# An attention layer with a gated feed-forward, one core: the next batch's values due after its keys, other due times, shift rows moved between engines, and four smaller edits

## The chip, the cores and the metric

One core of a Trainium2 chip. TensorE (PE) multiplies matrices, VectorE (DVE), ScalarE (ACT) and GpSimd (POOL) work on rows, SyncE (SP) issues every transfer of this kernel. Each engine takes its instructions in the order of the program and waits on semaphores for the others. The metric is the device time of one execution in microseconds, the median of several runs; lower is better.

## The reference

x is 8 batches of 2048 tokens by 512 channels, all in fp32.

```python
xn = layernorm(x)
q, k, v = xn @ Wq.T + bq, xn @ Wk.T + bk, xn @ Wv.T + bv      # 8 heads: 8, 8 and 64 wide
scores = einsum("bmhd,bnhd->bhmn", q, k) / sqrt(8)
scores = where(scores >= 0, scores, 0.2 * scores)
s = gamma * (softmax(scores, -1) @ v) + xn
base = xn @ W.T
proj = l2norm(xn @ Wp.T + bp)
lw = softmax(proj @ l2norm(sim) * scale)                       # 4 experts, ranks 1, 2, 4, 8
res = sum over e of (lw[e] if e is the largest else 0) * (xn @ Wd[e].T @ Wu[e].T)
out = x + s * silu(base + res)
```

## The kernel before

**Main loop.** The work is cut into sequences of 16 steps. A sequence is one pair of heads (of 4) and one block of 512 query tokens (of 4) of one batch, so a batch has 16 sequences (`SEQ`) and the program 128 of them, 2048 steps. A step takes one chunk of 128 key tokens. On TensorE a step holds `less_max` (L621, adds the negative row maximum to the scores), `score` of the next step (L604), `max_unit` (L546, plain scores of the next sequence but one, for their row maxima) and `weigh` (L643, probabilities by values). ScalarE does `leaky` (L618, Prelu in place) and `exp` (L635), VectorE the maximum of `max_unit` (L568), GpSimd `add_up` (L661), which sums the probabilities. `less_max` of a step needs `leaky` of its scores, `exp` needs `less_max`. Up to four `weigh` calls are put off and wait in the list `last`.

**Background.** Everything else is written as Python generators that yield after small pieces, and `background` (L775) is called once a step to issue some of them. Queue 2 holds the work of `behind` (L753): `project_block` (L334) makes keys, queries and values of one block of the next batch, `lift_block` (L382) the gated feed-forward of one block of this batch. Queue 0 holds `ending` (L671), which finishes a sequence: sums, division, transposition, product and output. Queue 1 holds `shift_rows` (L570), which turns the row maxima of the next sequence into the rows that `less_max` adds. A generator that yields HOLD or WAIT keeps the one PSUM bank that all of them share, and the others stand back. FREE, SLOW and WAIT end the call; IDLE passes one step. Each piece calls `spend` with its planned cost (`MM` = 0.86 for a matmul with 512 columns).

**Due times.** `tasks` (L726 to L744) gives every block a planned cost and a due time in sequences, and `due_at` (L746) turns them into the cost that should be spent by a given step. `background` stops when `spent` reaches it. One batch in the order of the list: lift 1, lift 2, project 0, project 1, lift 3, project 2, project 3 and lift 0 of the next batch. The first seven are due at 13.4 sequences (`AHEAD`), the last at 16. In the last batch only three lifts are left, due at 13.2 (`LAST`).

**Where the plan meets the main loop.** `load_stacks(s + 2)` at step 0 of a sequence loads keys and queries of the sequence after the next. If they belong to the next batch, it calls `background(force=True)` until that batch is in `ready`, and `ready` is set after the values of its last block. `load_values(s + 1)` comes at step 6. `ending` waits in IDLE until its block is in `lifted`. All transfers go through SP's queue in program order: the stores of KS, QS, XN, XT, VS and GS, the loads of k, q_sb, v_sb, gs and xs, the shift rows and the output.

```python
while b > 0 and b not in ready:          # load_stacks
    background(force=True)
```

**Before the loop** a prologue makes batch 0's keys and values and the first half of its first lift.

Of the kernel before, what the change touches and what calls it, by code (L numbers as in the profile page):

```python
# [20 lines left out]
BLK = 512  # L21
NT = BLK // 128
# [3 lines left out]
SLOPE = 0.2  # L26
# [6 lines left out]
def fused_layer_kernel(  # L33
# [37 lines left out]
    nc = tc.nc  # L71
    B, M, C = x.shape
    NC = C // 128
# [67 lines left out]
    def filled(name, value, dtype=FP):  # L141
        c = const.tile([128, 1], dtype, name=name)
        nc.gpsimd.memset(c, value)
        return c

    hi_bits = filled("hi_bits", HI_BITS, I32)
    minus_one = filled("minus_one", -1.0)
    ln_eps = filled("ln_eps", LN_EPS)

    kst = []  # L150
# [89 lines left out]
    def spend(cost):  # L240
        spent[0] += cost

    def project(ps, wt, xnT):
        for c in range(NC):
            if c:
                yield HOLD
            nc.tensor.matmul(ps, lhsT=wt[:, c, :], rhs=xnT[c], start=(c == 0), stop=(c == NC - 1))  # L247
            spend(MM)

    def token_major(ps, wt, xnT, t, more=False):  # L250
        for c in range(NC):
            if c:
                yield HOLD
            nc.tensor.matmul(  # L254
                ps,
                lhsT=xnT[c][:, t * 128 : (t + 1) * 128],
                rhs=wt[:, c, :],
                start=(c == 0),
                stop=(c == NC - 1 and not more),
            )  # L260
            spend(MM)

    def columns(*tiles):
        return [a[:, c, :] for a in tiles for c in range(a.shape[1])]

    normed = {}
    ready = []
    lifted = []
    fetched = {}

# [63 lines left out]
    def project_block(b, n, following, prefetch):  # L334

        if (b, n) not in normed:
            for _ in norm(b, n):
                pass
        xn, normalize = normed.pop((b, n))
        xnT = two.tile([128, NC, BLK], FP, name="xnT")  # L340
        for t in range(NT):
            tp = bank([128, NC, 128], "tp")
            for c in range(NC):
                nc.tensor.transpose(tp[:, c, :], xn[:, t, c * 128 : (c + 1) * 128], ident)
            if t + 1 < NT:
                normalize(t + 1)
            nc.vector.tensor_copy(xnT[:, :, t * 128 : (t + 1) * 128], tp)
            spend(0.5)
            yield FREE
        if prefetch:  # L350
            fetch(*prefetch)
        nxt = b * NB + n + 2
        if nxt < B * NB:
            load_x(nxt // NB, nxt % NB)

        ps = bank([128, BLK], "qkps")
        yield from project(ps, wqk_sb, columns(xnT))
        nc.scalar.activation(ps, ps, AF.Identity, bias=bqk_sb)
        yield WAIT
        hi = one.tile([128, BLK], FP, name="hi")  # L360
        lo = one.tile([128, BLK], FP, name="lo")
        split_keys(b, n, ps, hi, lo)
        nc.sync.dma_start(out=XN[b][n], in_=xn)
        nc.sync.dma_start(out=XT[b][n], in_=xnT)
        yield FREE

        vb = one.tile([128, NPAIR, NT, 128], FP, name="vb")
        for t in range(NT):
            ps = bank([128, C], "vps")
            yield from token_major(ps, wv_sb, columns(xnT), t)  # L370
            add_bias(vb, t, ps)
            next(following, None)
            yield FREE
        store_values(b, n, vb)
        if n == NB - 1:
            ready.append(b)
        if not prefetch:
            for _ in following:
                yield FREE
            yield FREE  # L380

    def lift_block(b, n, following, prefetch, cols=None):  # L382

        early = cols is not None
        if not early:
            if (b, n) not in fetched:
# [4 lines left out]

        ps = bank([128, BLK], "pps")
        yield from project(ps, wp_sb, cols)
        pw = one.tile([128, 2, BLK], FP, name="pw")
        nc.vector.tensor_scalar(pw[:, 0, :], ps, bp_sb, None, ALU.add)
        nc.scalar.activation(pw[:, 1, :], ps, AF.Square, bias=bp_sb)
        yield FREE
        nps = bank([128, NT], "nps")
        for t in range(NT):
            nc.tensor.matmul(  # L400
                nps[:, t : t + 1],
                lhsT=pw[:, 1, t * 128 : (t + 1) * 128],
                rhs=ones[:, 0:1],
                start=True,
                stop=True,
            )
# [13 lines left out]
        for t in range(NT):  # L420
            nc.tensor.matmul(
                gps[:, t, 0:NEXP],
                lhsT=pw[:, 0, t * 128 : (t + 1) * 128],
                rhs=simn,
                start=True,
                stop=True,
            )
# [75 lines left out]
    def where(s):  # L503
        return s // SEQ, s % NPAIR, (s % SEQ) // NPAIR
# [28 lines left out]
    def load_values(s):  # L533
        if s >= B * SEQ:
            return
        b, p, n = where(s)
        vts[s] = two.tile([128, CH, 128], FP, name="v_sb")
        nc.sync.dma_start(out=vts[s], in_=VS[b][p])

# [30 lines left out]
    def shift_rows(s):  # L570
        if s >= B * SEQ:
            return
        m = sm.tile([128, 2 * NT, 1], FP, name="m")
        nc.vector.reduce_max(m, mxr.pop(s).rearrange("p e t n -> p (e t) n"), axis=AX.X)
        yield IDLE

        ml = sm.tile([128, 2 * NT], FP, name="ml")
        nc.scalar.activation(ml, m[:, :, 0], AF.Prelu, alpha=SLOPE)
        c = sm.tile([128, 2, 2 * NT], FP, name="c")
        big = sm.tile([128, 2 * NT], FP, name="big")  # L580
        nc.scalar.activation(big, ml, AF.Copy, scale=-4097.0)
        nc.scalar.activation(ml, ml, AF.Copy, scale=-1.0)  # L582
        nc.gpsimd.tensor_tensor(c[:, 1, :], big, ml, ALU.subtract)  # L583
        nc.gpsimd.tensor_tensor(c[:, 0, :], big, c[:, 1, :], ALU.subtract)
        nc.gpsimd.tensor_tensor(c[:, 1, :], ml, c[:, 0, :], ALU.subtract)
        for _ in range(2):
            yield IDLE
        yield FREE
        cps = ps_m.tile([4 * NT, 128], FP, name="cps", tag="m")
        nc.tensor.transpose(cps, c.rearrange("p i m -> p (i m)"), ident)  # L590
        cT = sm.tile([4 * NT, 128], FP, name="cT")
        nc.vector.tensor_copy(cT, cps)
        spend(0.45)
        shift = qp.tile([128, BLK], FR, name="shift")
# [76 lines left out]
    def ending(s):  # L671
# [4 lines left out]
        nc.vector.tensor_copy(avs, avt.pop(s))  # L676
        yield IDLE
        sums = acc.pop(s)
        for _ in range(2):
            yield IDLE  # L680
        while (b, n) not in lifted:
            yield IDLE
        gs = two.tile([128, NT, 128], FP, name="gs")
# [35 lines left out]
        nc.sync.dma_start(out=ov[b, n][:, :, cols], in_=gs)  # L719
        yield FREE  # L720

    AHEAD = 13.4
    LAST = 13.2


    A1, A2 = 20 * MM + 2.0, 24 * MM + 3.7  # L726
    tasks = [(lift_block, 0, 0, 16 * MM + 1.7, 1.4)]
    for b in range(B):
        order = [(lift_block, b, 1)]
        if b + 1 < B:  # L730
            order += [(lift_block, b, 2), (project_block, b + 1, 0), (project_block, b + 1, 1)]
            order += [(lift_block, b, 3), (project_block, b + 1, 2), (project_block, b + 1, 3)]
            order += [(lift_block, b + 1, 0)]
        else:
            order += [(lift_block, b, 2), (lift_block, b, 3)]
        costs = [A2 if f is lift_block else A1 for f, _, _ in order]
        t0 = tasks[-1][4]
        steady = sum(costs) - (costs[-1] if b + 1 < B else 0.0)
        t1 = SEQ * b + (AHEAD if b + 1 < B else LAST)
        run = 0.0  # L740
        for k, (f, bb, n) in enumerate(order):
            run += costs[k]
            end = t0 + (t1 - t0) * run / steady if run <= steady + 0.01 else SEQ * (b + 1.0)
            tasks.append((f, bb, n, costs[k], end))  # L744

    def due_at(h):  # L746
        w, t = h * END, 0.0
# [3 lines left out]
        return w  # L751

    def behind():  # L753
        for k, (f, b, n, _, _) in enumerate(tasks):
            g, bb, nn = (tasks[k + 1] if k + 1 < len(tasks) else (None, 0, 0))[:3]
            following = norm(bb, nn) if g is project_block else iter(())
            if k == 0:
                yield from opening
            else:
                yield from f(b, n, following, (bb, nn) if g is lift_block else None)  # L760
# [48 lines left out]
    with tc.manual_schedule():  # L809
# [144 lines left out]
        for s in range(B * SEQ):  # L954
            for i in range(CH):
                if i == 0:
                    load_stacks(s + 2)
                if i == 6:
                    load_values(s + 1)
                due[0] = due_at(s + (i + 1) / CH)  # L960
                u = s * CH + i + CH + LEAD
# [82 lines left out]
```

## Time and profile before

| | before |
|---|---|
| median of 3 runs | 5834.28 us (5829.07 to 5840.97) |
| profiled execution, whole | 5841.93 us |
| its span | 5840.2 us |
| mean granted clock of TensorE | 0.967 |
| TensorE busy | 5433.9 us |
| GpSimd busy | 4705.6 us |
| ScalarE busy | 4276.0 us |
| VectorE busy | 3620.9 us |
| first L626 (step 0) | 132.5 us after the start |

The profile is one execution, taken on the chip. Busy time is counted per engine; matmuls overlap, so their sum can be more than the busy time. The timeline gives the start and duration of instructions, how many of a kind follow one another (x2), and in brackets how long the engine had been idle and what ended it. A table of windows gives for each stretch its length, the busy time of PE, its weight loads, DVE, ACT and POOL with their instructions, the granted clock, the DMA share and GB/s. A matmul in fp32 shows as two instructions.

### The profile page before, as it was taken

Reading aid. Unit: us, or ns where it says so; the run is one execution under the profiler, and the core shown is the slowest. Engines: PE = TensorE matmul, PEld = TensorE weight load, DVE = VectorE, ACT = ScalarE, POOL = GpSimd, SP = SyncE. Lnnn points to the kernel's source line nnn. Section 1 sums busy time; section 2 is a strip of 40 time slices with the busy share of each in tenths; the row PEclk is TensorE's granted clock in tenths of the full one; section 3 lists DMA queues with packets and bytes.
Section 4 is the critical chain, followed back from the end, with each engine's and each line's share of the span. In section 5 each row is a group of like instructions: output and inputs, shape, how many; then the busy total and the mean of one; then the engine's idle time right before and its main releaser. Section 6 shows DMA issues by size and latency. Waiting matters only on the chain.

```text
span 5840.2 us, 74003 instructions
## 1 busy us (share of the span) xinstructions
PE 5433.9 (93%) x26242; PEld 1780.7 (30%) x26242; DVE 3620.9 (62%) x4716; ACT 4276.0 (73%) x4915; POOL 4705.6 (81%) x2519
## 2 busy tenths in 40 slices
PE   7899999999999999999999999999999999988888
PEld 3333333333333333333333333333333333322222
DVE  5566656666566666666666666666666666555552
ACT  2677767777777777777777777777777777767666
POOL 1788878888888888888888888888888888878777
PEclk9999999999999999999999999999999999988885
DMA  5233333334224242243423434233342334322221
GB/s 200 90 109 121 105 115 88 108 106 152 89 75 152 77 152 86 75 143 95 135 82 95 132 104 130 82 104 123 104 124 89 104 111 129 97 62 80 70 76 33
DMA packets 517991, 614.04 MB, mean 105 GB/s; under 512 B 30780, under 2 KB 429116, under 8 KB 481528
## 3 DMA queue, kind: packets, MB, share of 16 engines
q1 hardware_dynamic: 517624, 609.32, 33.6%
q8 instruction: 209, 3.42, 0.2%
q14 instruction: 158, 1.29, 0.1%
HBM read 405.79 MB, written 201.33 MB: 104 GB/s over the span
## 4 chain that ended last, share of the span: by engine, by line
PE 68%; ACT 21%; DVE 5%; POOL 2%; issue 2%; DMA 1%; SPq 1%; ACTq 0%; POOLq 0%; DVEq 0%
PE av L649 22%; PE sc L626 14%; ACT ex L637 10%; ACT sc L619 9%; PE zps L254 9%; PE vps L254 8%; PE mx L561 5%; PE dps L247 2%; PE pps L247 2%; PE qkps L247 2%; DVE mxr L568 2%; POOL acc L669 1%; ACT xn L292 1%; PE sc L609 1%; DVE bs L277 1%
## 5 line engine op out<-in xcount | busy, mean ns | idle before, releaser
L669 POOL TENSOR_TENSOR acc<-acc,ex 128x1024 f32<-128x1024 f32 x1792 | 4236.9, 2364 | 353.0 <-ACT ex L637 268.3
L568 DVE TENSOR_REDUCE mxr<-mx 128x2 f32<-128x1024 f32 x2048 | 2504.2, 1223 | 1814.3 <-PE mx L561 1798.2
L637 ACT ACTIVATE ex<-sc 128x1024 f32<-128x1024 f32 x2048 | 2097.6, 1024 | 1388.2 <-PE sc L609 1198.7
L649 PE MATMUL av<-ex,v_sb 128*64 128x512 f32 x8192 | 2228.5, 634 | 0.9 <-DVE avs L676 0.9
L619 ACT ACTIVATE sc<-sc 128x1024 f32<-128x1024 f32 x2048 | 2086.2, 1019 | 19.9 <-PE sc L609 19.9
L626 PE MATMUL sc<-shift,ones_r 2*128 2x512 f32 x4096 | 1055.6, 507 | 301.6 <-ACT sc L619 294.3
L609 PE MATMUL sc<-q_sb,k 32*128 32x512 f32 x4096 | 1044.8, 506 | 0.0
L626 PEld LDWEIGHTS sc<-shift,ones_r 2*128 2x128 f32 x4096 | 393.9, 185 | 2050.2 <-ACT sc L619 1947.2
L561 PE MATMUL mx<-k,q_sb 32*128 32x512 f32 x4096 | 831.5, 400 | 13.5 <-DVE mxr L568 13.5
L649 PEld LDWEIGHTS av<-ex,v_sb 128*64 128x64 f32 x8192 | 437.9, 138 | 954.9 <-issue 928.6
L669 POOL TENSOR_TENSOR acc<-ex 128x1024 f32<-128x1024 f32 x128 | 301.9, 2358 | 397.6 <-ACT ex L637 397.6
L254 PE MATMUL zps<-w_sb,xnT 128*128 128x512 f32 x1024 | 567.4, 656 | 12.1 <-DMA xnT<-XT 12.0
L254 PE MATMUL vps<-wv_sb,xnT 128*128 128x512 f32 x960 | 508.3, 633 | 6.8 <-DVE vb L322 2.3
L561 PEld LDWEIGHTS mx<-k,q_sb 32*128 32x128 f32 x4096 | 400.3, 190 | 35.3 <-DVE mxr L568 33.9
L609 PEld LDWEIGHTS sc<-q_sb,k 32*128 32x128 f32 x4096 | 386.6, 186 | 0.8 <-issue 0.8
L254 PEld LDWEIGHTS zps<-w_sb,xnT 128*128 128x128 f32 x1024 | 168.3, 195 | 254.0 <-issue 194.8
L254 PEld LDWEIGHTS vps<-wv_sb,xnT 128*128 128x128 f32 x960 | 153.8, 189 | 210.9 <-issue 176.5
L492 DVE SCALAR_TENSOR_TENSOR g<-th,zps 128x512 f32<-128x512 f32 x128 | 88.0, 688 | 166.9 <-ACT th L491 166.9
L583 POOL TENSOR_TENSOR c<-big,ml 128x8 f32<-128x8 f32 x128 | 26.1, 204 | 186.8 <-ACT ml L582 178.8
L247 PE MATMUL pps<-xnT,wp_sb 128*128 128x512 f32 x256 | 142.1, 646 | 5.6 <-DVE vb L322 5.5
L247 PE MATMUL dps<-xnT,wd_sb 128*128 128x512 f32 x256 | 146.3, 661 | 0.1
L247 PE MATMUL qkps<-xnT,wqk_sb 128*128 128x512 f32 x240 | 123.4, 640 | 2.5 <-ACT xnT L842 1.4
(121 smaller groups left out, 2558.8 us busy)
## 6 DMA issues: line engine op xcount, KB each, us to landing
v_sb<-VS SPq DMA_DIRECT2D x127, 1024.0 KB
k<-KS SPq DMA_DIRECT2D x256, 256.0 KB
XN<-xn SPq DMA_DIRECT2D x32, 1024.0 KB
q_sb<-QS SPq DMA_DIRECT2D x256, 128.0 KB
xnT<-XT SPq DMA_DIRECT2D x32, 1024.0 KB
GS<-g SPq DMA_DIRECT2D x32, 1024.0 KB
gs<-GS SPq DMA_DIRECT2D x128, 256.0 KB
xs<-in_x_dram SPq DMA_DIRECT2D x128, 256.0 KB
```

The source lines that it names most:

```text
L247: nc.tensor.matmul(ps, lhsT=wt[:, c, :], rhs=xnT[c], start=(c == 0), stop=(c == NC - 1))
L254: nc.tensor.matmul(ps, lhsT=xnT[c][:, t * 128 : (t + 1) * 128], rhs=wt[:, c, :], start=(c == 0), stop=(c == NC - 1 and not more),)
L277: nc.vector.bn_stats(bs, xt[:, t, :])
L492: nc.vector.scalar_tensor_tensor(g[:, t, :], th, 1.0, ps, ALU.add, ALU.mult)
L561: nc.tensor.matmul(mx[:, e, :], lhsT=q_sb[r, t * 128 : (t + 1) * 128], rhs=k_sb[r, kb // 2 * BLK : (kb // 2 + 1) * BLK], start=True, stop= ...
L568: nc.vector.reduce_max(mxr[s][:, :, t, kb : kb + 1], mx, axis=AX.X)
L609: nc.tensor.matmul(sc[:, e, :], lhsT=k_sb[r, i // 2 * 128 : (i // 2 + 1) * 128], rhs=q_sb[r, :], start=True, stop=True,)
L619: nc.scalar.activation(sc, sc, AF.Prelu, alpha=SLOPE)
L626: nc.tensor.matmul(sc[:, e, :], lhsT=ones_r[r, :], rhs=shifts[s][r, :], start=False, stop=True, skip_group_check=True,)
L637: nc.scalar.activation(ex, sc, AF.Exp, scale=qscale)
L649: nc.tensor.matmul(avt[s][64 * e : 64 * e + DV, :], lhsT=v_sb[:, i, 64 * e : 64 * e + DV], rhs=ex[:, e, :], start=(i == 0), stop=(i == CH ...
L669: nc.gpsimd.tensor_tensor(acc[s], old, ex, ALU.add)
```

## The change

- **Due times.** `ready` is set after the keys of a batch's last block are on their way, and a second list, `valued`, after its values. Keys are due at 13.8 sequences, the last block's values (16 matmuls, an entry without a function) at 15.0, and block 0's lift of the next batch at 1.3 sequences into that batch. The last batch's three lifts are due at 13.5. `load_values` waits for `valued` and comes at step 6, or later, up to step 13, where it forces the background.
- **Shift rows.** Prelu and two scalings on ScalarE are replaced: VectorE makes min(m, 0) x 0.2 and max(m, 0), GpSimd adds them and does the two scalings, ahead of its three instructions of before.
- **Endings** pass two steps fewer before they load.
- **Gate.** The biased projection and its square are two tiles instead of one, and the square is issued first.
- **Fine pieces.** In lifts 1 to 3 of the last batch each matmul with 512 columns is issued as two with 256, with a yield between them.

```diff
-        nc.scalar.activation(ml, m[:, :, 0], AF.Prelu, alpha=SLOPE)
-        nc.scalar.activation(big, ml, AF.Copy, scale=-4097.0)
-        nc.scalar.activation(ml, ml, AF.Copy, scale=-1.0)
+        nc.vector.tensor_scalar(big, m[:, :, 0], 0.0, SLOPE, ALU.min, ALU.mult)
+        nc.vector.tensor_scalar_max(m[:, :, 0], m[:, :, 0], 0.0)
+        nc.gpsimd.tensor_tensor(ml, m[:, :, 0], big, ALU.add)
+        nc.gpsimd.tensor_tensor(big, ml, splitter.to_broadcast([128, 2 * NT]), ALU.mult)
+        nc.gpsimd.tensor_tensor(ml, ml, minus_one.to_broadcast([128, 2 * NT]), ALU.mult)
         nc.gpsimd.tensor_tensor(c[:, 1, :], big, ml, ALU.subtract)
...
+    fine = [False]
+    def pieces():
+        if fine[0]:
+            return [slice(0, BLK // 2), slice(BLK // 2, BLK)]
+        return [slice(0, BLK)]
     def project(ps, wt, xnT):
         for c in range(NC):
+            for part in pieces():
+                if c or part.start:
+                    yield HOLD
...
+                spend(MM / len(pieces()))
...
     def project_block(b, n, following, prefetch):
...
         nc.sync.dma_start(out=XT[b][n], in_=xnT)
+        if n == NB - 1:
+            ready.append(b)
         yield FREE
...
         if n == NB - 1:
-            ready.append(b)
+            valued.append(b)
...
     def lift_block(b, n, following, prefetch, cols=None):
+        fine[0] = b == B - 1 and n > 0
...
-        pw = one.tile([128, 2, BLK], FP, name="pw")
-        nc.vector.tensor_scalar(pw[:, 0, :], ps, bp_sb, None, ALU.add)
-        nc.scalar.activation(pw[:, 1, :], ps, AF.Square, bias=bp_sb)
+        pw = one.tile([128, BLK], FP, name="pw")
+        pw2 = one.tile([128, BLK], FP, name="pw2")
+        nc.scalar.activation(pw2, ps, AF.Square, bias=bp_sb)
+        nc.vector.tensor_scalar(pw, ps, bp_sb, None, ALU.add)
...
     def load_values(s):
+        while b not in valued:
+            background(force=True)
...
     def ending(s):
         sums = acc.pop(s)
-        for _ in range(2):
-            yield IDLE
...
-    AHEAD = 13.4
-    LAST = 13.2
-    tasks = [(lift_block, 0, 0, 16 * MM + 1.7, 1.4)]
+    A1, A2, LIFTED, KEYED, VALUED = 20 * MM + 2.0, 24 * MM + 3.7, 1.3, 13.8, 15.0
+    LAST = 13.5
+    tasks = [(lift_block, 0, 0, 16 * MM + 1.7, LIFTED)]
...
+        total = sum(o[3] for o in order) - (16 * MM if b + 1 < B else 0.0)
+        t0, run = SEQ * b + LIFTED, 0.0
+        for f, bb, n, cost in order:
+            run += cost
+            at = min(run / total, 1.0) * ((KEYED if b + 1 < B else LAST) - LIFTED) + t0
+            if run > total + 0.01:
+                tasks.append((f, bb, n, cost - 16 * MM, at))
+                tasks.append((None, bb, n, 16 * MM, SEQ * b + VALUED))
+            else:
+                tasks.append((f, bb, n, cost, at))
+        if b + 1 < B:
+            tasks.append((lift_block, b + 1, 0, A2, SEQ * (b + 1) + LIFTED))
...
-                if i == 6:
+                if i >= 6 and s + 1 not in vts and (where(s + 1)[0] in valued or i == 13):
                     load_values(s + 1)
```

More of the change, by code (lines that the diff above doesn't have):

```diff
@@ L147, in fused_layer_kernel @@
     minus_one = filled("minus_one", -1.0)
+    splitter = filled("splitter", -4097.0)
     ln_eps = filled("ln_eps", LN_EPS)
@@ L241, in spend @@
         spent[0] += cost
+    fine = [False]
[3 more added lines that the diff above has]
+        return [slice(0, BLK)]
     def project(ps, wt, xnT):
         for c in range(NC):
[L245 to L248, printed above, removed]
+            for part in pieces():
+                if c or part.start:
+                    yield HOLD
+                nc.tensor.matmul(
+                    ps[:, part],
+                    lhsT=wt[:, c, :],
+                    rhs=xnT[c][:, part],
+                    start=(c == 0 and part.start == 0),
+                    stop=(c == NC - 1 and part.stop == BLK),
+                )
+                spend(MM / len(pieces()))
     def token_major(ps, wt, xnT, t, more=False):
         for c in range(NC):
[L252 to L261, printed above, removed]
+            for part in pieces():
+                if c or part.start:
+                    yield HOLD
+                nc.tensor.matmul(
+                    ps[:, part],
+                    lhsT=xnT[c][:, t * 128 : (t + 1) * 128],
+                    rhs=wt[:, c, part],
+                    start=(c == 0 and part.start == 0),
+                    stop=(c == NC - 1 and part.stop == BLK and not more),
+                )
+                spend(MM / len(pieces()))
     def columns(*tiles):
@@ L267, in fused_layer_kernel @@
     ready = []
+    valued = [0]
     lifted = []
@@ L401, in lift_block @@
                 nps[:, t : t + 1],
-                lhsT=pw[:, 1, t * 128 : (t + 1) * 128],
+                lhsT=pw2[:, t * 128 : (t + 1) * 128],
                 rhs=ones[:, 0:1],
@@ L422, in lift_block @@
                 gps[:, t, 0:NEXP],
-                lhsT=pw[:, 0, t * 128 : (t + 1) * 128],
+                lhsT=pw[:, t * 128 : (t + 1) * 128],
                 rhs=simn,
@@ L720, in ending @@
         yield FREE
-    AHEAD = 13.4
-    LAST = 13.2
-    A1, A2 = 20 * MM + 2.0, 24 * MM + 3.7
-    tasks = [(lift_block, 0, 0, 16 * MM + 1.7, 1.4)]
+    A1, A2, LIFTED, KEYED, VALUED = 20 * MM + 2.0, 24 * MM + 3.7, 1.3, 13.8, 15.0
+    LAST = 13.5
+    tasks = [(lift_block, 0, 0, 16 * MM + 1.7, LIFTED)]
     for b in range(B):
-        order = [(lift_block, b, 1)]
+        order = [(lift_block, b, 1, A2), (lift_block, b, 2, A2)]
         if b + 1 < B:
-            order += [(lift_block, b, 2), (project_block, b + 1, 0), (project_block, b + 1, 1)]
-            order += [(lift_block, b, 3), (project_block, b + 1, 2), (project_block, b + 1, 3)]
-            order += [(lift_block, b + 1, 0)]
-        else:
[L735 to L744, printed above, removed]
+            order += [(project_block, b + 1, 0, A1), (project_block, b + 1, 1, A1), (lift_block, b, 3, A2)]
+            order += [(project_block, b + 1, 2, A1), (project_block, b + 1, 3, A1)]
+        else:
+            order += [(lift_block, b, 3, A2)]
+        total = sum(o[3] for o in order) - (16 * MM if b + 1 < B else 0.0)
[10 more added lines that the diff above has]
+            tasks.append((lift_block, b + 1, 0, A2, SEQ * (b + 1) + LIFTED))
     def due_at(h):
@@ L753, in behind @@
     def behind():
-        for k, (f, b, n, _, _) in enumerate(tasks):
-            g, bb, nn = (tasks[k + 1] if k + 1 < len(tasks) else (None, 0, 0))[:3]
+        jobs = [t for t in tasks if t[0]]
+        for k, (f, b, n, _, _) in enumerate(jobs):
+            g, bb, nn = (jobs[k + 1] if k + 1 < len(jobs) else (None, 0, 0))[:3]
             following = norm(bb, nn) if g is project_block else iter(())
```

## The prediction

> **What bounds the kernel now.** I read the page first, then the timeline of one ordinary stretch, then the joints between batches, then the stages. The page: TensorE is busy 93% of the span, ScalarE and GpSimd follow, and the granted clock sags at the end only.
>
> ```profile
> PE 5433.9 (93%) x26242; PEld 1780.7 (30%) x26242; DVE 3620.9 (62%) x4716; ACT 4276.0 (73%) x4915; POOL 4705.6 (81%) x2519
> PEclk9999999999999999999999999999999999988885
> PE 68%; ACT 21%; DVE 5%; POOL 2%; issue 2%; DMA 1%; SPq 1%; ACTq 0%; POOLq 0%; DVEq 0%
> ```
>
> A step runs from one less_max pair (L626) to the next. Steps have two floors. Around the ScalarE loop: 0.63 us from L626 to the Exp, 0.92 until the Prelu starts, 1.02 for it, 0.05 to the next L626 = 2.62. On TensorE: 0.66 (less_max, scores, maxima), 1.05 for a background matmul with its switch (0.86 each when they follow one another), 1.01 for a weigh = 2.73. In the timeline, first a step with one matmul and one weigh (2.73), then the joint of a batch: two value matmuls, a wait on their bias, two gate matmuls, and ScalarE idle 5.50 us; this step lasts 1481.32-1473.91 = 7.41.
>
> ```profile
> 1471.18 0.50 PE L626 MATMUL sc<-shift,ones_r 2*128 2x512 f32 x2
> 1473.91 0.50 PE L626 MATMUL sc<-shift,ones_r 2*128 2x512 f32 x2
> 1479.41 1.98 PE L247 MATMUL pps<-xnT,wp_sb 128*128 128x512 f32 x4 [0.79 <-DVE vb L322]
> 1481.32 0.50 PE L626 MATMUL sc<-shift,ones_r 2*128 2x512 f32 x2
> 1481.97 1.02 ACT L637 ACTIVATE ex<-sc 128x1024 f32<-128x1024 f32 x1 [5.50 <-PE sc L609]
> ```
>
> That is load_stacks forcing the background. The first joint forces most of a block; its step lasts 784.37-754.28 = 30.09:
>
> ```profile
> 756.93 3.70 PE L247 MATMUL qkps<-xnT,wqk_sb 128*128 128x512 f32 x8 [0.26 <-DVE xnT L347]
> 762.83 5.40 PE L254 MATMUL vps<-wv_sb,xnT 128*128 128x512 f32 x8 [2.20 <-DVE lo L308]
> ```
>
> The 5.40 against 3.70 is a slow clock after a pause. Stages: batch 5 whole, then sequences 0, 1, 2 and 10 of the last batch (the figure after the last bracket is the clock). With half the background the last batch should be at the ScalarE floor, 16 x 2.62 = 42; sequence 1 takes 54.6 at clock 0.62.
>
> ```profile
> 3676.70:4376.40 699.70, 661.02 (x3282) 216.75 (x3280) 452.26 (x588) 533.33 (x613) 587.28 (x313) 1.00 0.36 109
> 5081.80:5124.50 42.70, 40.51 (x211) 12.78 (x209) 25.49 (x29) 32.78 (x38) 36.77 (x21) 1.00 0.29 96
> 5124.50:5179.10 54.60, 51.68 (x192) 16.58 (x190) 28.68 (x45) 32.57 (x39) 36.56 (x19) 0.62 0.27 77
> 5179.10:5221.80 42.70, 35.57 (x190) 10.61 (x188) 25.34 (x28) 32.12 (x37) 35.31 (x19) 1.00 0.22 67
> 5545.50:5597.90 52.40, 49.31 (x196) 15.90 (x196) 29.55 (x46) 32.80 (x39) 36.24 (x19) 0.71 0.24 68
> ```
>
> [...] the clock records are 1.0 or 0.5, in multiples of 3.41 us. Of warm windows under 70% busy 19 of 40 were followed by a cold one, of the others 7 of 1506. [...]
>
> **The change, part by part.** I replayed the planner's own bookkeeping (due times, `spent`, yields) for both versions. For the kernel before, the background's lag behind its due time comes out as in the trace sequence by sequence (10.3 units at the end of sequence 12), so I trust the placement; durations are the trace's.
>
> *Joints.* The lag, not the due time, decides what load_stacks(16(b+1)) finds undone. Before: two value matmuls plus two of the next task, 7.41-2.65 = 4.76 us in six joints, 27.4 in the first: 56. After: LIFTED at 1.3 moves lift (b,0) into the new batch, so as much stands before the keys as the values free, and the background is 8.7 units late at the joint. The whole head of the last block is forced: four transposes and the keys. From L626: 2.6 until the weighs end, normalised rows at 3.4, four rounds of transposes 0.66, copy 0.68 (L347) and hand-overs 0.1 = 5.8, keys 3.70: 12.9, or 10.2 over a step. In 6.6 us of it TensorE is 40% busy, so the clock should fall: spells in batches 0 to 6 average 5.9 us, and a cold step takes 4.86 for 2.73 (timeline after 5168.7), so 0.44 x 5.9 = 2.6, with 0.75 chance 2.0. 7 x 12.2 = 85: **+29**.
>
> Behind it on SP stand eight KS/QS stores (0.6 each), XN and XT (1.3), k (2.3), q (1.8). The split ends 1.4 us after the keys; the last q issue is 12 us after them, and 2.75 MB at 300 GB/s (the stretches after 1482 moved 255 to 319) from the XN issue are down at 15.5. Their first reader, the maxima of the new batch, comes 7 steps = 19 us later: hidden by 3.5 us; without it, each us costs 7. The later values: VS store at 15.0, v_sb load in step 6 of sequence 15, first weigh ten steps on, nothing. GS of block 0 is stored four steps before its ending needs it; SP may wait 4.3 us (the longest such wait) ahead of the xs loads, whose use is four steps, 10.7 us, later: nothing, at most 2 us x 7.
>
> *Even pace and the two waits.* Counts of steps in batches 0 to 6 by content, before to after, with the trace's mean: matmul+weigh 597 to 524 (2.743), two weighs 261 to 306 (2.648), two matmuls 219 to 255 (2.639), weigh+transposes 111 to 84 (2.608), matmul+weigh+L488 71 to 54 (2.958), weigh alone 62 to 86 (2.631), two matmuls+L488 45 to 58 (2.807), L468 one less: **-10**. The waits are in these counts: sums, two transposes and the output go two steps earlier, and the three loads with them, with the same distance from load to use. The sums (L694) then come three to six steps after the last Exp; GpSimd is under 1.5 us late there in nine of ten sequences, so TensorE does not wait; without that cover, up to 1 us x 127.
>
> *Shift rows.* The three ScalarE instructions (0.19+0.21+0.21, 0.7 with gaps) mostly lie in ScalarE's pause before the Exp and cost nothing. Where a normalise (0.80) shares the pause they do:
>
> ```profile
> 1067.42 0.21 ACT L582 ACTIVATE ml<-ml 128x8 f32<-128x8 f32 x1
> 1067.53 0.80 ACT L292 ACTIVATE xn<-xt,nmr,rstd 128x512 f32<-128x512 f32 x1
> 1070.21 0.49 PE L626 MATMUL sc<-shift,ones_r 2*128 2x512 f32 x2 [0.81 <-ACT sc L619]
> ```
>
> 24 such steps, 0.49 each over the usual: **-12**. VectorE gains two instructions (about 0.16 each, as L197 and L408), GpSimd three (0.20 as L583, 0.28 with gaps). GpSimd waits in order for VectorE's result[...]; GpSimd was not waiting for ScalarE at 46 of 128 shifts, so it is sometimes late. VectorE has about 2 us before its maximum (L568, one buffer) holds TensorE. Bounds 0 and +45, I take **+4**. The transpose of c comes 5.4 us or more after the step's L626 and c is ready at about 4.2.
>
> *Gate's square.* ScalarE no longer follows VectorE on one tile. "ACT pw <- DVE pw" is 14.0, 6.9 of it once; the 28 steps with L400 stand 0.16 above their median: **-5**.
>
> *Last batch.* Half matmuls cost 0.43 and the same 0.2 of switching (estimate from L254): 0.66+0.63+1.01 = 2.30, under the floor, so splitting is free while warm; the extra weight loads (0.19) overlap. Sequences 1 to 12 stand 51 us above 12 x 42.5. Sequence 1 (12 of them) now carries the end of lift (7,0): -11. In the rest, clusters of bare weigh steps remain around the gate; by the 70% rule the cold starts fall by a fifth: 0.22 x 39. Sequences 13 to 15 stay bare. **-20**; bounds 0 and -50.
>
> Sum: 29-10-12+4-5-20 = -14, against the profiled execution (5841.9, span 5840.2). That stands 7.6 over the median of the runs; the difference goes to the median: 5834.3-14 = 5820.
>
> **Rivals.** *Warm last batch*: even halves keep every window over 70%; for it, sequences 0, 2 and 9 ran at clock 1.00; against, the bare clusters. -50 there instead of -20: 5790. *Nothing in the last batch*: 5841. *The joint is worse* (slower than before): the pause sends TensorE cold for ten us and more, as in sequence 9 of batch 3 (13.7 us), and the keys run at half speed. Each joint then costs 17: +34, 5855. The change gains nothing from 14.2 us per joint on and loses 0.2% from 15.8; for it the 40% busy stretch, against the short spells. [...]
>
> **How the numbers follow.** As summed (5808 to 5834): 0.40, a little over half of it beyond 0.2%, which is 11.7 us and about what can be told from no change. Warm 0.20, nothing 0.17, worse joint 0.15, lock-out 0.08. Faster 0.23+0.20 = 0.43; same 0.17+0.17 = 0.34; slower 0.23. The range 5782 to 5864 leaves out the tails of the warm case and of the lock-out.
>
> **What would show it.** Joints: steps of 13 to 16 us with four copies out of tp (L347 before) and 3.7 us or more of qkps ahead of L626, the clock at 0.5 there. The first L561 of a new batch without a DMA wait. L583 no longer released by ScalarE, L292 no longer behind small ScalarE work. Last batch about 725 us instead of 744, sequence 1 near 43. I am wrong if the joints are short (the lag is not what I replayed), if L568 is held up after shift rows, or if the last batch's clock stays as it was.

## The result, and where the time went

The changed kernel takes 5982.7 us (median of 4 runs, 5959.4 to 5999.4) against 5831.7 (5828.1 to 5841.0): a ratio of 1.0245, interval 1.0208 to 1.0282. The forecast was 5820. The profiled execution has a span of 5957.6 us against 5840.2, 117.4 more. It is the shortest of the four; the medians lie 151 apart, and what the other 34 us are no trace shows.

The page of the changed kernel: engine busy time, the granted clock by slices, and the chain of waits by engine and by line.

```profile
PE 5472.5 (92%) x26386; PEld 1834.0 (31%) x26386; DVE 3655.2 (61%) x4972; ACT 4212.7 (71%) x4531; POOL 4784.2 (80%) x2904
PEclk9999999899999999999999999999999999999986
PE 64%; ACT 20%; DVE 7%; DMA 3%; issue 3%; SPq 1%; POOL 1%; ACTq 0%; POOLq 0%; DVEq 0%
PE av L675 20%; PE sc L652 13%; ACT ex L663 9%; ACT sc L645 9%; PE vps L271 8%; PE zps L271 8%; PE mx L585 5%; PE qkps L257 2%; DVE mxr L592 2%; PE dps L257 2%; PE pps L257 2%; DMA xs<-XN 2%; ACT xn L310 1%; POOL acc L695 1%; SPq L549 1%
```

TensorE works only 39 us more. DMA grew on the chain from 1% to 3%, and one transfer is now named, which the list by line had not before: the load `xs<-XN` of the endings. The windows of batch 5, of the last batch's sequences 1, 2 and 10, and of the whole last batch (columns as before; the figure after the last bracket is the clock):

```profile
3772.00:4499.90 727.90, 678.75 (x3280) 224.61 (x3280) 456.92 (x621) 525.54 (x564) 596.36 (x361) 0.96 0.35 105
5266.40:5309.50 43.10, 40.45 (x220) 14.44 (x218) 25.81 (x31) 32.15 (x34) 36.43 (x23) 1.00 0.38 121
5309.50:5357.00 47.50, 43.07 (x203) 15.88 (x204) 28.75 (x47) 32.23 (x35) 37.79 (x23) 0.82 0.21 63
5668.10:5717.10 49.00, 44.64 (x203) 15.53 (x201) 28.75 (x47) 31.73 (x35) 36.38 (x22) 0.77 0.21 63
5222.50:5943.20 720.70, 644.56 (x3111) 218.78 (x3111) 387.94 (x505) 508.80 (x539) 585.61 (x336) 0.87 0.23 70
```

Batch 5 grew from 699.7 to 727.9 at clock 0.96 where it had 1.00; the last batch fell from 743.9 to 720.7. Taken sequence by sequence over batches 0 to 6, after minus before (rounded):

| | us |
|---|---|
| sequence 13 (its last step is the joint's forced stretch) | +38 |
| sequence 14 | +83 |
| sequence 15 | +14 |
| sequence 4 | +25 |
| the twelve others together | -17 |
| last batch | -23 |
| time before step 0 | -2 |
| sum | +117 |

So 134 us lie in three sequences at each joint. The timeline of one joint, from the forced step on:

```profile
1478.73 0.50 PE L652 MATMUL sc<-shift,ones_r 2*128 2x512 f32 x2
1482.07 0.65 PE L362 MATMUL tp<-ident,xn 128*128 128x128 f32 x4 [0.73 <-ACT xn L310]
1488.78 5.35 PE L257 MATMUL qkps<-xnT,wqk_sb 128*128 128x512 f32 x8 [0.78 <-DVE xnT L365]
1494.06 0.50 PE L652 MATMUL sc<-shift,ones_r 2*128 2x512 f32 x2
1501.20 0.46 SPq L381 DMA_DIRECT2D XN<-xn  x1
1502.54 2.97 SPq L543 DMA_DIRECT2D k<-KS  x2
1505.55 3.15 SPq L549 DMA_DIRECT2D q_sb<-QS  x2
1510.06 1.41 SPq L711 DMA_DIRECT2D xs<-XN  x1
1510.59 0.50 PE L652 MATMUL sc<-shift,ones_r 2*128 2x512 f32 x2
1517.71 0.70 DVE L738 TENSOR_TENSOR atp<-atp,xs 128x512 f32<-128x512 f32 x1 [9.76 <-DMA xs<-XN]
1519.59 0.80 PE L585 MATMUL mx<-k,q_sb 32*128 32x512 f32 x2 [8.50 <-DVE mxr L592]
1524.64 0.79 PE L652 MATMUL sc<-shift,ones_r 2*128 2x512 f32 x2
```

There are two stalls. The forced step runs from 1478.73 to 1494.06, 15.3 us; over the seven joints it takes 15.3 to 15.9, together 35 more than before. The second begins six steps after its end: step 6 of sequence 14 lasts 14.05 us here, 12.7 to 14.0 at the seven joints, and was 2.6 or 2.7 before: together +74. VectorE stands in `ending` at the addition of xs; behind it in its queue stands the maximum (L592), and behind that TensorE's next maxima (L585). Note where SP is: VectorE was ready for xs at 1507.95 (1517.71 - 9.76), but SP, still going through stores and then k and q, gave the load out at 1510.06. The waits over the whole run (us in total, times, longest):

```profile
DVE atp L738 <- DMA xs<-XN: 64.0, 7, 9.8
PE mx L585 <- DVE mxr L592: 61.9, 33, 8.5
DVE pw L418 <- ACT pw L417: 37.9, 32, 3.4
```

### The profile page after: what moved, and what is told of

The parts are those of the page before. It is cut to its first block, busy times and chain, and to the rows that moved or that the text cites. A ratio compares the mean times of both kernels' runs of the same rounds, so it can differ in the third digit from the quotient of the medians.

```text
span 5957.6 us, 74790 instructions
## 1 busy us (share of the span) xinstructions
PE 5472.5 (92%) x26386; PEld 1834.0 (31%) x26386; DVE 3655.2 (61%) x4972; ACT 4212.7 (71%) x4531; POOL 4784.2 (80%) x2904
## 4 chain that ended last, share of the span: by engine, by line
PE 64%; ACT 20%; DVE 7%; DMA 3%; issue 3%; SPq 1%; POOL 1%; ACTq 0%; POOLq 0%; DVEq 0%
PE av L675 20%; PE sc L652 13%; ACT ex L663 9%; ACT sc L645 9%; PE vps L271 8%; PE zps L271 8%; PE mx L585 5%; PE qkps L257 2%; DVE mxr L592 2%; PE dps L257 2%; PE pps L257 2%; DMA xs<-XN 2%; ACT xn L310 1%; POOL acc L695 1%; SPq L549 1%
## 5 line engine op out<-in xcount | busy, mean ns | idle before, releaser
L592 DVE TENSOR_REDUCE mxr<-mx 128x2 f32<-128x1024 f32 x2048 | 2503.2, 1223 | 1730.0 <-PE mx L585 1712.0
L585 PE MATMUL mx<-k,q_sb 32*128 32x512 f32 x4096 | 833.2, 401 | 61.9 <-DVE mxr L592 61.9
L271 PE MATMUL zps<-w_sb,xnT 128*128 128x512 f32 (+1 forms) x1120 | 567.2, 616 | 12.9 <-DMA xnT<-XT 10.8
L271 PE MATMUL vps<-wv_sb,xnT 128*128 128x512 f32 x960 | 526.3, 648 | 9.9 <-DVE gs L742 3.8
L585 PEld LDWEIGHTS mx<-k,q_sb 32*128 32x128 f32 x4096 | 402.4, 190 | 78.5 <-DVE mxr L592 76.6
L271 PEld LDWEIGHTS zps<-w_sb,xnT 128*128 128x128 f32 x1120 | 189.4, 196 | 256.0 <-issue 201.4
L606 POOL TENSOR_TENSOR ml<-m,big 128x8 f32<-128x8 f32 x128 | 26.2, 205 | 249.5 <-DVE m L605 243.8
L257 PE MATMUL dps<-xnT,wd_sb 128*128 128x512 f32 (+1 forms) x280 | 147.9, 636 | 0.0
L257 PE MATMUL pps<-xnT,wp_sb 128*128 128x512 f32 (+1 forms) x280 | 137.1, 593 | 3.3 <-DVE gs L742 3.0
```

What stands on the lines that cost most here:

```text
L257: nc.tensor.matmul(ps[:, part], lhsT=wt[:, c, :], rhs=xnT[c][:, part], start=(c == 0 and part.start == 0), stop=(c == NC - 1 and part.stop ...
L271: nc.tensor.matmul(ps[:, part], lhsT=xnT[c][:, t * 128 : (t + 1) * 128], rhs=wt[:, c, part], start=(c == 0 and part.start == 0), stop=(c = ...
L585: nc.tensor.matmul(mx[:, e, :], lhsT=q_sb[r, t * 128 : (t + 1) * 128], rhs=k_sb[r, kb // 2 * BLK : (kb // 2 + 1) * BLK], start=True, stop= ...
L592: nc.vector.reduce_max(mxr[s][:, :, t, kb : kb + 1], mx, axis=AX.X)
```

## The experiments

Two theories at the start. *Joints*: nearly all of the loss is at the joints, because the due times force the last block's head and crowd the transfers; with the old due times it goes. *Distance*: the loss is in how soon an ending uses xs after a block's stores; the two removed waits did that, and it would show wherever a block's keys are split. Steps are named (sequence, step), both counted from 0.

**1. The last block's XN and XT stored later** (changed kernel)

```diff
-        nc.sync.dma_start(out=XN[b][n], in_=xn)
-        nc.sync.dma_start(out=XT[b][n], in_=xnT)
+        if n < NB - 1: ...the same two here
...
+            if n == NB - 1 and t == 1: ...the same two, after the second value tile
```

> The changed kernel with one edit: the stores of XN and XT of a batch's last block are issued after the second value tile instead of before the first. Theory (transfer queue): at each of the 7 joints the three loads of the ending stand on SP's queue and in the DMA engines behind 2 MB of stores, so the addition of xs waits 9 us; with the stores later, step 6 of sequence 14 falls from about 13.4 us to 3 to 6, the forced step at the end of sequence 13 stays at 15 to 16, and the time falls by 45 to 75 us, to 5908 to 5938. Rival (issue time): what delays the loads is the row of KS, QS, k and q issues on SP, not the two stores; then only their 1.2 us of issue go, the step stays above 11.5 and the time above 5965.

Measured: 5924.9 us, 1.0159 (1.0124 to 1.0195). The seven waits for xs fall from 64.0 to 20.6 us and step (14,6) to 5.0 to 8.2; the forced steps stay at 14.3 to 16.8. The stores ahead of the load are a cause, but not the only one. Of the 6.2 us saved at each joint, SP accounts for 4.4 (the load goes out that much sooner, measured against the moment when VectorE is ready) and the transfer for 1.8: the load lands 5.2 to 6.4 us after it was given out, where it was 7.1 to 7.7.

**2. The two waits put back** (changed kernel)

```diff
         sums = acc.pop(s)
+        for _ in range(2):
+            yield IDLE
```

> The changed kernel with the two waits put back into the endings. Theory (transfer queue): loads and use both come two steps, about 5.3 us, later, while the queue in front of them stays, so the wait of 9 us at each joint shrinks to about 4, step 6 (now 8) of sequence 14 to about 8, and the time falls by 35 to 60 us, to 5923 to 5948. Rival (the waits do nothing at the joints, the endings only moved): within 15 us of 5983. Forced step at the joint: 4.4 planned units instead of 5.4, about 14 us.

Measured: 5903.8 us, 1.0122 (1.0091 to 1.0152). It gained some 79 us, more than expected; the waits for xs at the joint fall to 3.3 to 4.3 each, 26.3 together. That is one part of the gain. Another is in the forced steps, which take 9.9 to 12.8 us in place of 15.3 to 15.9, 31 less over the seven joints: with the two waits in, one of the four rounds of transposes and one weigh are no longer part of them. Of all parts the two waits, costed at nothing in the prediction, are the dearest.

**3. Due times earlier, so that less is forced** (changed kernel)

```diff
-    ... LIFTED, KEYED, VALUED = ..., 1.3, 13.8, 15.0
+    ... LIFTED, KEYED, VALUED = ..., 0.8, 13.4, 15.0
```

> The changed kernel with two numbers changed: block 0's lift is due at 0.8 instead of 1.3 sequences, the keys at 13.4 instead of 13.8. By the planner's arithmetic nothing is forced at the joints any more (the keys end in step 15 of sequence 13 by themselves). Theory (forced stretch plus transfer queue): the step at the end of sequence 13 falls from 15.6 to about 2.7 us, the wait for xs stays but is 2 to 3 us shorter, so sequence 13 takes 43 to 45, sequence 14 about 50 to 52, and the time falls by 105 to 140 us, to 5843 to 5878. Rival (the pace itself, and the colder clock it brings, cost the time, not the joint): above 5930.

Measured: 5925.3 us, 1.0173 (1.0140 to 1.0205). A miss. Sequence 13 did come down to 46.2 us, but the waits for xs remained, 11 of them, 63.6 us: in batches 1, 3 and 5 at (14,6), steps of 13.5 to 14.7, and in 0, 2, 4 and 6 at (8,7) and (12,7), steps of 8.5 to 9.1. It lies between the two ranges, so neither theory is borne out. Take them away at one place and they come at another.

**4. The old due times** (changed kernel, with `tasks` and the place of `ready.append` as before)

> The changed kernel with the due times of before, and ready set after the values as before; endings, shift rows, gate and fine pieces stay changed. Theory (all the loss is at the joints): joints as before (7.4 us, the first 30), no wait for xs, last batch about 720 instead of 744; less about 12 us lost in the gate: 5790 to 5815, faster than before. Rival (shift rows on GpSimd and VectorE, or the earlier endings, cost too): above 5831.

Measured: 6012.6 us, 1.0312 (1.0284 to 1.0340), slower still. The *joints* theory fell. Twelve waits for xs, 51.2 us, now at (7,7) and (11,7), where two of the four blocks are split under the old plan.

**5. The due times alone** (kernel before, with the new `tasks`, `ready`, `valued` and the value load's condition)

> The kernel before with the new due times, the value load's condition and the early start of the endings' batch switch, and nothing else: the endings keep their two waits, the shift rows stay on ScalarE, the gate and the last batch are as before. Queue theory (a use of xs comes too soon after the last split's stores; two of its steps come from the waits removed, the rest from the due times): seven forced stretches of 14 to 16 us where before had one of 27 and six of 5, +30 to +35; at the same joints xs <- XN makes VectorE wait 2 to 4 us each and the step takes 5 to 8 us in place of 2.7, +20 to +35; cold clock after it, +15 to +30. Sum 5890 to 5925. The rival that the due times cost only what the forced stretch adds: 5850 to 5865. The rival that the loss is in the endings and not in the due times: 5815 to 5830.

Measured: 5883.2 us, 1.0085 (1.0060 to 1.0110), just under the low end. The forced steps were 9.9 to 11.6 at the seven joints, shorter than expected, and 73 us together, no more than before (75); the seven waits for xs 2.7 to 3.5, 21.6 us together, as expected.

**6. The endings alone** (kernel before, without the two waits)

```diff
         sums = acc.pop(s)
-        for _ in range(2):
-            yield IDLE
```

> The kernel before without the two waits in each ending, and nothing else. Queue theory: the uses of xs come two steps, some 5.3 us, nearer to the stores of the split before them, so that at two of four splits in a batch the wait for xs <- XN appears, 3 to 5 us of VectorE and a step of 8 to 9 us in place of 2.7: 15 x 5 to 6 = +75 to +90, and colder clock after them, together 5895 to 5980. The recorded prediction's view (the waits hold nothing up, and their removal costs nothing): 5815 to 5835.

Measured: 5947.8 us, 1.0196 (1.0173 to 1.0219). One line of the waits:

```profile
DVE atp L712 <- DMA xs<-XN: 53.6, 12, 4.7
```

Steps (7,7) and (11,7) take 8.1 to 9.2 us in each of batches 1 to 6, the places and the size expected. Sequence 7 of batch 1, first in the kernel before, then here: the load goes out 4.5 and 4.1 us after the store of XN, and the use comes 11.5 us after the load in the one; in the other VectorE is ready 4.15 us after it and waits 4.47 more.

```profile
1182.50 0.46 SPq L363 DMA_DIRECT2D XN<-xn  x1
1187.00 2.04 SPq L687 DMA_DIRECT2D xs<-XN  x1
1198.54 0.70 DVE L714 TENSOR_TENSOR atp<-atp,xs 128x512 f32<-128x512 f32 x1
```

```profile
1194.15 0.45 SPq L363 DMA_DIRECT2D XN<-xn  x1
1198.25 2.53 SPq L685 DMA_DIRECT2D xs<-XN  x1
1206.87 0.70 DVE L712 TENSOR_TENSOR atp<-atp,xs 128x512 f32<-128x512 f32 x1 [4.47 <-DMA xs<-XN]
```

Two IDLE lines cost 2%, with no due time changed.

**7. The same, with the stores out of the way** (number 6, and in every block XN and XT stored after the second value tile)

> e10_endings_alone (kernel before without the two waits) with each block's two stores XN and XT given out after its second value tile, some 5 us later, so that the loads of xs can go ahead of them. Queue theory: the waits for xs <- XN of 3.6 to 4.7 us at steps (7,7) and (11,7) fall to below 1.5 us, those steps take 3 to 5 us in place of 9, and the time falls from 5948 to 5850 to 5900. If the endings' steps meet other work there and the stores have nothing to do with it: 5935 to 5960 as before the edit.

Measured: 5875.8 us, 1.0065 (1.0043 to 1.0087). The wait of VectorE is gone from the list; what is left of this transfer is

```profile
PE sc L627 <- DMA xs<-XN: 2.3, 4, 0.9
```

and steps (7,7) and (11,7) are back under 3 us. The same place as in number 6:

```profile
1190.38 0.62 SPq L686 DMA_DIRECT2D xs<-XN  x1
1197.22 0.70 DVE L713 TENSOR_TENSOR atp<-atp,xs 128x512 f32<-128x512 f32 x1
```

That shows where these waits come from: without the two waits, the stores of XN and XT stand ahead of a load that is soon needed. Some 70 of the 106 us of span that number 6 lost are gone with them. The rest, 35 us of span, lies elsewhere and is not explained: 19 us in the last batch, where no block is stored.

**8. Shift rows alone** (kernel before, with VectorE and GpSimd making them)

> The kernel before with the shift rows made by VectorE and GpSimd in place of ScalarE, and nothing else. Recorded prediction: 128 times 0.05 to 0.15 us off the steps, 5804 to 5818. If the changed kernel's steps got shorter for another reason (the removed waits, the due times): 5821 to 5826. [...]

Measured: 5923.2 us, 1.0139 (1.0110 to 1.0168): slower. Some of VectorE's new instructions are drawn out until a sum of GpSimd ends, which the changed kernel hardly shows (4 of 256). The timeline of a step in sequence 6 of batch 4:

```profile
3298.46 4.82 POOL L672 TENSOR_TENSOR acc<-acc,ex 128x1024 f32<-128x1024 f32 x2
3301.10 2.21 DVE L582 TENSOR_SCALAR m<-m 128x8 f32<-128x8 f32 x1
3303.23 0.68 DVE L348 COPY xnT<-tp 128x512 f32<-128x512 f32 x1
3304.05 0.64 PE L697 MATMUL dps<-acc,ones 128*32 128x256 f32 x8 [1.75 <-DVE xnT L348]
```

The VectorE instruction on 8 elements takes 0.17 us elsewhere; here it takes 2.21 and ends with GpSimd's sum. Of 256 such instructions 45 are longer than 0.25 us, 57.5 us together over their medians, and each of the 45 ends 0.03 us after the sum that was running. The copy of xnT waits behind it, and so TensorE's next user of that bank. Then the clock falls: steps (6,9) to (6,11) take 3.4, 4.1 and 4.7 us. Sequences 6, 9, 10 and 12 hold 70 of the 79 us of span, and in batches 0 to 6 the clock is at half for 256 us, against 89 before.

**9. The shift rows' two products on GpSimd, nothing on VectorE** (kernel before)

```diff
         nc.scalar.activation(ml, m[:, :, 0], AF.Prelu, alpha=SLOPE)
-        nc.scalar.activation(big, ml, AF.Copy, scale=-4097.0)
-        nc.scalar.activation(ml, ml, AF.Copy, scale=-1.0)
+        nc.gpsimd.tensor_tensor(big, ml, splitter.to_broadcast([128, 2 * NT]), ALU.mult)
+        nc.gpsimd.tensor_tensor(ml, ml, minus_one.to_broadcast([128, 2 * NT]), ALU.mult)
```

> The kernel before with two of the shift rows' three ScalarE instructions (the products with -4097 and -1) on GpSimd; Prelu stays on ScalarE, and VectorE gets nothing new. If what cost e6_shift_alone its time is VectorE's tensor_scalar waiting for GpSimd's running sums: no such wait is left, steps with a shift row get 0.03 to 0.08 us shorter, 5815 to 5832. If it is that the rows get ready later when GpSimd makes them: long steps in the same sequences as there, 5870 to 5920.

Measured: 5834.5 us, 1.0005 (0.9991 to 1.0020). No VectorE instruction is drawn out and the long steps are gone: the two VectorE instructions, with the addition on GpSimd that needs them, were the cost, not GpSimd's two products. A gain is not to be seen in the median either; in its profile the steps that run at full clock in both kernels are 7 us shorter together.

**10. The gate alone** (kernel before, square in its own tile and given out first)

> The kernel before with the gate's square in a tile of its own and given out ahead of VectorE's copy, and nothing else. If the two readings of the PSUM bank still follow one another, with ScalarE's square now first: VectorE's pw waits for ScalarE some 1.2 us in each of 32 blocks, and the step in which nps stands takes 0.3 to 0.5 us longer: 5831 to 5840. The recorded prediction's view (the two readings run side by side): 5815 to 5821.

Measured: 5891.0 us, 1.0096 (1.0071 to 1.0121): slower, and by more than expected. The profiled execution is the shortest of the six (5865.1), so the trace shows only 23 us of the loss: 14, 10 and 9 in sequences 2, 8 and 14, and 8 less in the last batch. The same block of batch 2, in the timeline of this kernel and then of the kernel before:

```profile
1674.13 1.02 ACT L620 ACTIVATE sc<-sc 128x1024 f32<-128x1024 f32 x1
1675.07 0.68 ACT L396 ACTIVATE pw<-pps,bp_sb 128x512 f32<-128x512 f32 x1
1675.78 0.75 DVE L397 TENSOR_SCALAR pw<-pps,bp_sb 128x512 f32<-128x512 f32 x1 [1.20 <-ACT pw L396]
1676.58 1.05 PE L401 MATMUL nps<-ones,pw 128*128 128x1 f32 x8 [0.54 <-DVE pw L397]
```

```profile
1672.38 0.74 DVE L395 TENSOR_SCALAR pw<-pps,bp_sb 128x512 f32<-128x512 f32 x1
1673.15 0.69 ACT L396 ACTIVATE pw<-pps,bp_sb 128x512 f32<-128x512 f32 x1
1673.89 1.05 PE L400 MATMUL nps<-ones,pw 128*128 128x1 f32 x8
```

The two readings of the bank still follow one another, with separate tiles. Before, VectorE read during ScalarE's Prelu, 1.92 us after the step's L626 (1670.46), and ScalarE came when both had ended. Now ScalarE is first, comes only after its Prelu (1674.13 to 1675.15), and VectorE waits for it. The matmuls that follow write into the same bank, and the program lets them wait for the later of the two ([0.54 <-DVE pw L397]): they start 3.99 us after the L627 of the step before theirs (1672.59), where it was 3.43 (1673.89 - 1670.46). Half a microsecond; but then the clock falls: the matmuls' step lasts 4.08 us and the next 5.06, where it was 2.7 each, and at this place it falls in four of batches 1 to 6. Why not in the other two, with the same stall, is not shown.

**11. Fine pieces in the last batch alone** (kernel before)

> The kernel before with the projections' matmuls of the last batch's three later liftings cut into two halves, and nothing else. Recorded prediction: 20 us off, all of them in the last batch (744 us before, about 724): 5803 to 5822. If the last batch's gain in the changed kernel came from another part: 5821 to 5835.

Measured: 5821.8 us, 0.9984 (0.9973 to 0.9995). The whole last batch in the windows, this kernel:

```profile
5067.90:5796.40 728.50, 657.28 (x3085) 219.61 (x3083) 379.39 (x465) 513.87 (x580) 575.88 (x291) 0.83 0.23 69
```

15 us less than before (743.9), of 20 forecast. That is one execution of each: the profile of number 12, with the same pieces, has 746.2 for this stretch. The medians, of 22 and 59 executions, are the firmer figure: 3 to 16 us less.

**12. Numbers 9 and 11 together**

> e12_shift_gpsimd and e8_fine_alone together on the kernel before. If the two do not disturb one another: the sum of their gains, 5795 to 5820, below the kernel before. If a few tenths of a us on GpSimd are enough to bring stalls elsewhere: above 5835.

Measured: 5824.7 us, 0.9983 (0.9970 to 0.9995). No more than number 11. Both are faster than the kernel before by less than 0.2%. The fine pieces are the only part of the change that gained by itself.

## Why the prediction was wrong

*Joints*: right. The forced step was forecast to hold the four rounds of transposes and the keys, and did; it was forecast at 12.2 us over a step and measured at 12.9; +35 against +29, and the clock fell to half in it (at the joint above from 1485.3 to 1492.1; eight keys matmuls in 5.35 us, not 3.70). The rival "the joint is worse", at 17 us each, did not come. But the two waits, which the prediction priced at nothing, are in this figure: with them in (numbers 2 and 5) the forced steps hold three rounds and take 9.9 to 12.8 us, about as much over the run as before.

*Behind it on SP*: incomplete. It followed what stands on SP as far as the new batch's first maxima, and no wait of theirs for a load is in the trace. It left out the ending of sequence 13, whose loads stand in the same queue behind it.

*Even pace and the two waits*: the step that failed, in the words "the three loads with them, with the same distance from load to use". The counts of steps came out (303 with two weighs where 306 were forecast, 84 with a weigh and transposes where 84 were), but not this distance. In number 6 VectorE is ready for xs three steps sooner than before at (7,7) and five at (11,7), and the load goes out at the same step or one sooner: SP gives it out behind the stores. It goes out 4 to 5 us after the XN store and lands 7.5 to 8.6 us later, as the VectorE instructions that waited for it show. With the waits in, the use came 11.3 us or more after such a load; without them, VectorE stands ready 3 to 4 us after it. In the changed kernel, at the joint, VectorE stands ready before the load is out at all. Predicted nothing, measured +74 in the step that waits, and with the steps at half speed after it most of sequence 14's +83. Numbers 1, 2, 6 and 7 show it from both sides.

The pace itself: the twelve quiet sequences gained 17 us, where pace, shift rows and gate were to give 10 + 12 - 4 + 5 = 23; but sequence 4 lost 25 and sequence 15 14. Number 5 has losses there too (22, with another 25 in sequence 5, and 15), so they belong to the new due times. In sequence 4 the clock is at half for 27.3 us in each of batches 1, 3 and 5. Ahead of it stand two steps with one weigh each and no background work, at whose ends TensorE waits for ScalarE:

```profile
1052.64 0.50 PE L652 MATMUL sc<-shift,ones_r 2*128 2x512 f32 x2 [0.87 <-ACT sc L645]
1055.25 0.79 PE L652 MATMUL sc<-shift,ones_r 2*128 2x512 f32 x2 [0.86 <-ACT sc L645]
```

These two steps are alike in batches 0 to 6 of the changed kernel and of number 5, and the clock falls behind them in ten of these fourteen cases. The clock records are multiples of 3.41 us long, and the stretches of 3.41 us between their edges tell the two kinds apart here: where one stretch held most of both pauses, TensorE was busy for 51 to 61% of it, and the clock fell each time; where they lay in two, busy for 68 to 72% of the emptier one, it never did. (The prediction's count for stretches under 70%, taken again from step 0 on, gives 23 of 43, and 5 of 1518 for the others: about the same. The line at 70% is the author's: a count, no rule.)

*Shift rows*: the gain is not cleanly shown. Steps with a weigh and the sums, at full clock, went from 2.72 to 2.64 us, 10 us over the run where 12 were forecast; but the endings moved these steps too. The forecast of +4, an estimate of the author's that no trace had shown, like its bound of +45 (the prediction's lock-out), came out in this kernel (4 of 256 instructions drawn out by 2.3 us together), by luck. The bound was too low: alone the same edit costs 1.4%, with 57.5 us of drawn-out instructions and the clock at half for 256 us in place of 89 (number 8). Only the position of the rows against GpSimd's sums, which the due times move, spared the changed kernel (numbers 3 and 4, with other due times, have 34 and 33 long ones).

*Gate's square*: wrong in sign. -5 forecast; the 28 steps with these matmuls rose from 2.90 to 3.32 us, +12. The step that failed here is "ScalarE no longer follows VectorE on one tile": with a tile each to write, what the two still share is the bank that both read. The wait is the program's: in all 32 blocks VectorE's instruction waits for the semaphore that ScalarE's raises at its end, as ScalarE's waited for VectorE's before.

*Last batch*: right in this execution, 720.7 against "about 725", sequence 1 at 43.1 against "near 43". Half of the gain is sequence 1, which also takes 43.3 with the due times alone; but among the kernels with the old plan it takes 44.1 to 54.6, so a single execution does not show much.

The parts do not add up: alone they give +0.85, +1.96, +1.39, +0.96 and -0.16%, together 5.0, and the whole is 2.45. In the whole, the new due times leave one place in a batch where xs is late, not two, and move the shift rows out from under the sums.

What stays open: why the clock falls after the gate's stall at some places and not at others; what number 7 still loses; and how the gate's two readings of one bank would run without the program's semaphore between them. That the load of xs is late both by SP's order and by its own slower transfer, number 1 shows; why the transfer is slower behind the stores, no run shows.

## What to carry to other kernels

A wait that "does nothing" may be the distance that a load needs. Before it is removed, find the load behind the use and everything that stands ahead of it on its queue; if that is fixed in time, moving the instruction that issues it hardly moves the load (number 6: VectorE ready three to five steps sooner, the load given out one sooner at most). And where the clock falls as easily as here, price a stall of half a microsecond with the steps at half clock that may follow it: at the gate of sequence 2 in batch 2 two steps cost 3.7 us more, for a stall of 0.56.

## What the runs showed of the hardware

- 45 of the 256 VectorE `tensor_scalar` instructions on 128x8 elements of number 8 took over 0.25 us, up to 2.2 in place of 0.17; each of the 45 ended 0.03 us after the GpSimd `tensor_tensor` that was running. In the changed kernel four of 256 started while a GpSimd `tensor_tensor` ran; these four alone were long (0.33 to 1.60 us), and each ended 0.03 us after it.
- A load of 256 KB, given out on SP's queue 4 to 5 us after the store of 1 MB that stands ahead of it, landed after 7.5 to 8.6 us (number 6). With the two stores given out later (number 7), the uses at these places came 5.5 to 6.8 us after the load and waited 0.1 us at most.
- In the gate, VectorE and ScalarE read one PSUM bank, and the program's semaphores put one reading after the other, whether the two wrote one tile or two. With ScalarE first, VectorE waited in 32 of 32 blocks (37.9 us in the changed kernel) and started 0.03 us after it; with VectorE first (the kernel before), ScalarE started 0.03 to 0.04 us after it in 31 of 32, but was busy until shortly before, and only 10 of its waits were longer than 0.15 us (14.0 us).
- The clock records read 1.0 or 0.5 and last multiples of 3.41 us, 63 of 64 before and 111 of 112 in the changed kernel (the last ends with the trace). After a stall of some 0.5 us on TensorE the clock was at half for 3.4 or 6.8 us at some places (number 10), after delays of some 2 us on VectorE for up to 13.7 (number 8). A stretch of 3.41 us in which TensorE was 51 to 61% busy was followed by half clock in ten of ten cases in sequence 4 (the changed kernel and number 5), one 68 to 72% busy in none of four. In batches 0 to 6 the slow spells add up to 324 us in the changed kernel and 89 before.
